# Bilinear samples on TensorE instead of VectorE for the first two chunks, and a convolution that follows its samples by thirds

## The chip, the cores and the metric

The kernel runs on one core of a Trainium2 chip. The metric is the device time of one execution in microseconds (us), as the median of several runs. A profile is one further execution, taken with the hardware profiler; the clock of the profile starts at the first instruction.

The core has five engines, each with its own queue that is worked off strictly in order. TensorE (PE in the views) multiplies matrices into PSUM; the loads of its stationary operands are listed apart as PEld. VectorE (DVE) does elementwise work and copies out of PSUM. ScalarE (ACT) computes exponentials. GpSimd (POOL) issues indirect DMAs here and computes a few small powers. SyncE (SP) issues nearly all other DMAs.

## The reference, cut to what matters

The input is four images of 128 channels and 64 x 64 pixels. Layer 0 is a deformable 3 x 3 convolution on the group-normalised image; the edited code is its sampling step:

```python
offset = conv2d(x, w_off, b_off)                    # 18 channels
mask = sigmoid(conv2d(x, w_mask, b_mask))           # 9 channels
py = base_y + ki + offset[:, 0::2];  px = base_x + kj + offset[:, 1::2]
y0 = floor(py);  x0 = floor(px);  wy = py - y0;  wx = px - x0
samples = (v00 * (1 - wy) * (1 - wx) + v01 * (1 - wy) * wx
           + v10 * wy * (1 - wx) + v11 * wy * wx) * mask   # v..: four corner pixels, 0 outside
x = x + einsum('bckhw,ock->bohw', samples, w_flat) + bias  # k: the 9 taps
```

Layer 1 takes the 4096 pixels of an image as tokens of 128 channels. It normalises them and runs an attention with 16 heads of 8 channels (queries, keys and values are the same ring products of cosines), a small feed-forward part, and a mixture of eight experts with the best two per token. Every token attends to all 4096 of its image:

```python
scores = einsum('bhsd,bhtd->bhst', q, q) / sqrt(8)
ctx = einsum('bhst,bhtd->bhsd', softmax(scores), q)
```

## The kernel before, in words

**Two streams.** The long part is attention, written as a list of steps (`steps`). One step takes 128 keys against 512 queries for a group of four heads: `scores` (L1261) puts a product in PSUM, ScalarE takes the exponential (L1270), and `context` (L1281) multiplies it with the values into `acc`. Beside it runs everything else, written as Python generators that yield what their next piece needs (`need`: TensorE time, VectorE time, a latency, whether it holds the PSUM bank, a time after which data have landed). A planner, the class `Beside`, keeps a modelled time for each engine and decides at build time in which order the pieces are put into the queues. The order of the instructions on TensorE, VectorE, SyncE and GpSimd is then exactly the order of emission (`tc.manual_schedule`). Before the first step is possible the planner is forced along (`force`); afterwards each attention step lets in as many pieces as fit (`step`).

**Preparation of an image.** An image has 8 chunks of 512 pixels, and a chunk has 4 blocks of 128. `prepare` loads the image, group-normalises it, writes a table of pixel pairs to DRAM (`corner_table`), computes offsets, indices `idx` and the four weights of each sample `wt` in two halves (`offsets`; the second half's index and weight part is the generator `rest`), and then runs `deform`.

**`deform`** (L599) walks over 96 units. A unit is one block and three of the nine taps; in a chunk the order is three taps for the four blocks, then the next three taps. Of each unit:

- `gather` (L625, three indirect DMAs on GpSimd) brings, for each tap, four corner pixels of 128 channels for each of 128 positions into the tile `v`. Up to unit 35 of image 0 gathers run four units ahead, with five buffers (three under the tag `v`, two under the tag `et`, taken by `spare`).
- L645: VectorE multiplies `v` with the weights `wt`, 1536 elements a partition. L650 and L651 add the four corners, 768 and 384 elements.
- In chunks 0 and 1 of image 0, TensorE transposes the three samples (L662) into a PSUM tile `sT_ps`, and VectorE copies it into `sT_first` (L665, the function `move`, emitted one unit later). In all other chunks VectorE transposes 32 x 32 blocks and the samples go through DRAM (`smd`, L686 and L698).

**`convolved`** (L719) follows when a chunk's twelve units are done: nine taps in two halves of 256 columns, each split into four matmuls of 32 output rows (`by_columns`, L281), added up in one PSUM tile `conv_ps`. Then come the bias and the residual `xr` (L758), a transposition, and `features`: layer norm statistics, a power on GpSimd (`rstd`, L396), the normalised tokens (L788), cosines and ring products on VectorE (L811 to L822), a copy on GpSimd (`fx`, L823), a transposition and a split in two parts (L836 to L839), and the DMAs that put keys, queries and values into DRAM, from where attention loads them. For image 0 attention begins as soon as chunk 0's tokens are there and goes on as further chunks come in.

**PSUM.** `misc` hands out one bank to all pieces, except while the list `alone` is filled, that is until chunk 0 is prepared and again at the very end; then it takes from the three buffers that scores use otherwise.

Of the kernel before, what the change touches and what calls it, by code (L numbers as in the profile page):

```python
# [9 lines left out]
F32 = mybir.dt.float32  # L10
# [3 lines left out]
ALU = mybir.AluOpType  # L14
# [8 lines left out]
P = 128  # L23
C = 128
# [6 lines left out]
KK = 9  # L31
# [16 lines left out]
NST = 3  # L48
# [151 lines left out]
FREE = -1.0  # L200


def need(pe=0.0, dve=0.0, lat=0.0, hold=False, after=0.0):

    return pe, dve, lat, hold, after


def ve(n, ops=1):  # L210

    return ops * (0.17 + n / 960.0)


MM256 = 0.44
MM128 = 0.23


def tr(n):

    return 0.13 + 0.115 * n
# [3 lines left out]
def kernel(  # L225
# [22 lines left out]
    nc = tc.nc  # L248
# [350 lines left out]
    def deform(b, tab, idx, wt, rest):  # L599
# [12 lines left out]
        def gather(last):  # L612

            nonlocal issued
            while issued < len(units) and issued <= last + (4 if early(issued) else 2):
# [12 lines left out]
                    )  # L628
                ahead.append((v, beside.gathered()))

        sent = 0.0
        moved = []
        gather(-1)
        for n, (ch, kg, j) in enumerate(units):
# [6 lines left out]
            v, landed = ahead.pop(0)  # L641
            v4 = v.rearrange("p k (q c) -> p (k q) c", c=C)
            w12 = wt[:, j, 3 * kg : 3 * kg + 3, :].rearrange("p k q -> p (k q)")
            yield need(dve=ve(1536), after=landed)
            nc.vector.tensor_tensor(v4, v4, w12[:, :, None].to_broadcast([P, 12, C]), ALU.mult)  # L645
            if moved:
                yield need(pe=0.01, dve=ve(384))
                moved.pop()()
            yield need(dve=ve(768) + ve(384))
            nc.vector.tensor_tensor(v[:, :, : 2 * C], v[:, :, : 2 * C], v[:, :, 2 * C :], ALU.add)  # L650
            nc.vector.tensor_tensor(v[:, :, :C], v[:, :, :C], v[:, :, C : 2 * C], ALU.add)  # L651
            if b == 0 and ch < 2:


                if n % 12 == 0:
                    while len(summed) < ch:
                        yield need(lat=0.5)
                    sT = big.tile([P, KK, CH], F32, tag="xs", name=f"sT_first{ch}")
                yield need(pe=tr(3), lat=FREE, hold=True)
                pt = misc(f"sT_ps{j}_{kg}")  # L660
                for k in range(3):
                    nc.tensor.transpose(pt[:, P * k : P * (k + 1)], v[:, k, :C], ident)  # L662

                def move(sT=sT, kg=kg, i=j % 4, pt=pt):
                    nc.vector.tensor_copy(  # L665
                        sT[:, 3 * kg : 3 * kg + 3, P * i : P * (i + 1)],
                        pt[:, : 3 * P].rearrange("p (k c) -> p k c", c=P),
                    )

                moved.append(move)  # L670
                beside.later(beside.now + 0.8, lambda n=n: gather(n))
                if n % 12 == 11:
                    yield need(pe=0.01, dve=ve(384))
                    moved.pop()()
                    featuring.append(True)
                    beside.add("prepare", convolved(b, ch, sT), 0.5, True)
                    if ch == 0:
                        yield from rest
                continue

            yield need(dve=ve(384))
            if j % 4 == 0:
                beside.flush(sent)
# [32 lines left out]
        while featuring:  # L716
            yield need(lat=1.0)

    def convolved(b, ch, sT=None):  # L719

        xr = work.tile([P, CH], F32, tag="p2", name=f"xr{b}_{ch}", bufs=NP2)
        nc.sync.dma_start(out=xr, in_=xf[b, :, CH * ch : CH * (ch + 1)])
# [13 lines left out]
        if not in_order:  # L736
# [1 line left out]
            yield need(lat=6.0)  # L738
            get(1)
            yield need(lat=4.0)  # L740
        for k in range(KK):
            if k == 2 and not in_order:
                get(2)
            for hf in range(2):
                last = k == KK - 1 and hf == 1
                yield need(pe=MM256, dve=ve(128, 4) if last else 0.0, lat=0.2 if last else FREE, hold=not last)
                if k == 0 and hf == 0:
                    po = misc(f"conv_ps{b}_{ch}")
                by_columns(
                    po[:, 256 * hf : 256 * (hf + 1)], wconv_sb[:, k, :],  # L750
                    sT[:, k, 256 * hf : 256 * (hf + 1)], k == 0 and hf == 0, last,
                )
# [815 lines left out]
```

## Time and profile before

| quantity | value |
|---|---|
| median of 3 runs | 7589.68 us (7587.77 to 7598.68) |
| profiled execution, time | 7632.52 us |
| its span, first to last instruction | 7630.7 us |
| busy PE, ACT, DVE, POOL | 93%, 90%, 59%, 22% of the span |
| first exponential | at 180.4 us |
| ScalarE busy, 200 to 400 us | 115 of 200 us |
| ScalarE busy, 700 to 900 us | 189 of 200 us |
| gathers, L625 | 1152, busy 1450.7 us |
| products, L645 | 384, mean 1735 ns |
| additions, L650 and L651 | 384 each, mean 956 and 562 ns |

In the page's groups a row gives line, engine, operation, output tile and input tiles, shapes, number, busy time, mean duration of one, and the idle time of the engine in front of them. In a timeline a row gives start, duration, engine, line, operation and number; the brackets hold the idle time ahead of it and what ended that. Two or more rows of one engine may be merged where they follow each other closely. Matmul records can be missing, so their numbers are lower bounds.

### The profile page before, as it was taken

To read this page: it belongs to the slowest core of one execution; us is meant where nothing else is said; L and a number is where in the kernel's file an instruction comes from. 1 tells how busy PE (TensorE), PEld (TensorE's weight loads), DVE (VectorE), ACT (ScalarE), POOL (GpSimd) and SP (SyncE) were. 2 spreads that over 40 slices of the span, in tenths; PEclk is the share of its full clock that TensorE was granted. 3 is DMA by queue.
4 is the path that set the end of the run, shared out by engine and by line. 5 is a ranking of instruction groups with operands and counts; after the bars stand their busy time and mean duration, and the time that the engine had idled before them with its cause. 6 is when DMAs were issued, how large, how long until landed. Compare 5 with 4: busy or idle time off the path is not lost.

```text
span 7630.7 us, 180510 instructions
## 1 busy us (share of the span) xinstructions
PE 7132.4 (93%) x73736; PEld 2383.1 (31%) x73736; DVE 4479.3 (59%) x8976; ACT 6855.1 (90%) x7441; POOL 1653.8 (22%) x1326
## 2 busy tenths in 40 slices
PE   3679899899999999999999999989999999999997
PEld 2122232223333333333333323323333333333333
DVE  6766356667444867776554677775444545455534
ACT  0569899899999999999999988989999999999995
POOL 5544034443000432422000334331000000000000
PEclk6889999999999999999999999999999999999998
DMA  6677567978445878887655688897554466667662
GB/s 176 208 212 222 137 209 238 302 235 295 151 172 196 289 231 268 282 273 239 203 179 185 232 274 287 286 309 251 184 175 162 148 232 230 234 217 244 222 204 64
DMA packets 909787, 1689.50 MB, mean 221 GB/s; under 512 B 150754, under 2 KB 384124, under 8 KB 858268
## 3 DMA queue, kind: packets, MB, share of 16 engines
q1 hardware_dynamic: 809102, 1371.37, 54.5%
q0 software_dynamic: 92160, 302.06, 12.5%
q8 instruction: 579, 9.49, 0.5%
q10 hardware_dynamic: 7694, 4.52, 0.2%
q14 instruction: 252, 2.06, 0.1%
HBM read 1027.51 MB, written 650.14 MB: 220 GB/s over the span
## 4 chain that ended last, share of the span: by engine, by line
PE 82%; DMA 8%; DVE 4%; issue 3%; ACT 2%; SPq 1%; POOL 1%; another core or an unknown queue 0%; ACTq 0%; POOLq 0%; DVEq 0%
PE acc L1281 40%; PE sc L1261 24%; PE acc L1214 5%; PE e_ps L281 4%; PE conv_ps L281 4%; DMA et<-etd 3%; PE f_ps L281 2%; ACT e L1270 2%; DMA sT<-smd 1%; PE om_ps L533 1%; DMA etd<-st 1%; DVE v L645 1%; DMA smd<-tr 1%; POOL v L625 0%; PE ao_ps L281 0%
## 5 line engine op out<-in xcount | busy, mean ns | idle before, releaser
L1270 ACT ACTIVATE e<-sc 128x1024 f32<-128x1024 f32 x7400 | 6852.0, 1076 | 637.9 <-PE sc L1261 456.3
L1281 PE MATMUL acc<-e,qf 128*9 128x512 f32 (+1 forms) x29600 | 3946.4, 602 | 33.8 <-DVE cu L1488 15.2
L1261 PE MATMUL sc<-qT,kT 32*128 32x512 f32 x14800 | 2380.9, 500 | 193.8 <-ACT e L1270 97.7
L1261 PEld LDWEIGHTS sc<-qT,kT 32*128 32x128 f32 x14800 | 948.2, 183 | 3663.1 <-ACT e L1270 3140.8
L625 POOL DMA_INDIRECT v<-tab,idx x1152 | 1450.7, 1259 | 1679.6 <-DVE tr L686 1058.0
L1140 DVE STREAM_TRANSPOSE st<-e 128x1024 f32<-128x1024 f32 x792 | 937.3, 1221 | 774.8 <-ACT e L1270 651.0
L1281 PEld LDWEIGHTS acc<-e,qf 128*9 128x9 f32 (+1 forms) x29600 | 682.3, 91 | 629.3 <-issue 345.8
L396 POOL TENSOR_TENSOR r<-ln_t,expo 128x4 f32<-128x4 f32 x96 | 112.2, 1170 | 3111.0 <-DVE ln_t L394 3073.8
L645 DVE TENSOR_TENSOR v<-v,wt 128x1536 f32<-128x1536 f32 x384 | 666.1, 1735 | 102.9 <-DMA v<-tab,idx 88.2
L1214 PE MATMUL acc<-et,qv 128*9 128x128 f32 x12672 | 509.2, 277 | 58.9 <-DMA et<-etd 45.5
L1065 DVE TENSOR_TENSOR eo<-e_ps,gt 128x512 f32<-128x512 f32 x256 | 175.2, 686 | 549.1 <-PE e_ps L281 540.3
L650 DVE TENSOR_TENSOR v<-v 128x768 f32<-128x768 f32 x384 | 367.1, 956 | 9.8
L281 PE MATMUL conv_ps<-sT,wconv_sb 128*32 128x256 f32 x4320 | 352.3, 400 | 11.0 <-DMA sT<-smd 8.8
L1214 PEld LDWEIGHTS acc<-et,qv 128*9 128x9 f32 x12672 | 270.8, 90 | 263.2 <-issue 220.9
L1486 DVE COPY cu<-acc 128x512 f32<-128x512 f32 x128 | 88.5, 691 | 349.0 <-PE acc L1281 290.5
L686 DVE STREAM_TRANSPOSE tr<-v 128x128 f32<-128x128 f32 x1080 | 249.3, 281 | 45.2 <-DMA etd<-st 36.5
L651 DVE TENSOR_TENSOR v<-v 128x384 f32<-128x384 f32 x384 | 215.7, 562 | 13.3
L396 POOL TENSOR_TENSOR rstd<-lt_t,expo 128x4 f32<-128x4 f32 x32 | 59.4, 1856 | 515.2 <-DVE lt_t L394 494.9
L281 PE MATMUL f_ps<-w_sb,h 128*32 128x128 f32 x4096 | 167.6, 282 | 1.5 <-issue 1.5
L950 DVE TENSOR_SCALAR h<-h_ps,b_sb 128x512 f32<-128x512 f32 x128 | 94.9, 744 | 100.3 <-PE h_ps L948 85.0
L823 POOL COPY fx<-rn 128x512 f32<-128x512 f32 x32 | 26.9, 840 | 535.2 <-DVE rn L822 338.2
L965 DVE TENSOR_TENSOR a<-a,f_ps 128x512 f32<-128x512 f32 x32 | 22.0, 686 | 202.9 <-PE f_ps L281 202.5
(224 smaller groups left out, 3148.5 us busy)
## 6 DMA issues: line engine op xcount, KB each, us to landing
etd<-st SPq DMA_DIRECT2D x396, 1024.0 KB
et<-etd SPq DMA_DIRECT2D x396, 1024.0 KB
kT<-kTd SPq DMA_DIRECT2D x372, 256.0 KB
smd<-tr SPq DMA_DIRECT2D x360, 192.0 KB
sT<-smd SPq DMA_DIRECT2D x360, 192.0 KB
qT<-qTd SPq DMA_DIRECT2D x166, 256.0 KB
atd<-cu SPq DMA_DIRECT2D x128, 256.0 KB
qf<-fqd SPq DMA_DIRECT2D x372, 72.0 KB
```

The lines of the kernel that those rows point to most:

```text
L281: nc.tensor.matmul(dst[c : c + 32], lhsT=lhsT[:, c : c + 32], rhs=rhs, start=start, stop=stop)
L625: nc.gpsimd.indirect_dma_start(out=v[:, k, :], out_offset=None, in_=tab, in_offset=bass.IndirectOffsetOnAxis(ap=idx[:, j, kk : kk + 1], ax ...
L645: nc.vector.tensor_tensor(v4, v4, w12[:, :, None].to_broadcast([P, 12, C]), ALU.mult)
L650: nc.vector.tensor_tensor(v[:, :, : 2 * C], v[:, :, : 2 * C], v[:, :, 2 * C :], ALU.add)
L651: nc.vector.tensor_tensor(v[:, :, :C], v[:, :, :C], v[:, :, C : 2 * C], ALU.add)
L686: nc.vector.transpose(out=tr9[:, k, :, j % 4, :], in_=v[:, k, :C].rearrange("p (c i) -> p c i", i=32),)
L1065: nc.vector.tensor_tensor(ws[hf], pe.rearrange("p (e c) -> p e c", c=C), gt[:, i, 4 * hf : 4 * (hf + 1), None].to_broadcast([P, 4, C]), AL ...
L1140: nc.vector.transpose(out=st[:, :, 2 * pr : 2 * pr + 2, :].rearrange("p o h (q j) -> p o (h q) j", j=32), in_=es[pr].rearrange("p h (q o i ...
L1214: nc.tensor.matmul(acc[32 * h : 32 * h + QW, P * kt : P * (kt + 1)], lhsT=qv[:, at : at + QW], rhs=e[:, :, h, 32 * t : 32 * (t + 1)], star ...
L1261: nc.tensor.matmul(ps[i // 2][:, i % 2, :], lhsT=kT[h : h + 32, P * (t % 4) : P * (t % 4 + 1)], rhs=qT[h : h + 32, :], start=True, stop=True,)
L1270: nc.scalar.activation(e, ps[pr], AF.Exp, scale=1.0 / math.sqrt(HD))
L1281: nc.tensor.matmul(acc[32 * h : 32 * h + width, :], lhsT=flat[:, first : first + width], rhs=es[h // 2][:, h % 2, :], start=(t == ts[0]), ...
```

## The change

For units 0 to 23 (image 0, chunks 0 and 1) VectorE no longer multiplies and adds the corners. It builds twelve diagonal matrices `dg`, identity times one corner's weights, in one instruction of 1536 elements; the tile has the tag `st` with three buffers. TensorE multiplies each corner's pixels with its diagonal matrix and adds the four corners of a tap in PSUM; the product comes out transposed already. Each of these multiplications is split in four column strips by `by_columns`.

In chunk 0 the convolution is taken out of `convolved` and goes along in thirds (`taps`): when three taps of all four blocks are copied, their six multiplications are emitted, into a PSUM tile `conv_first` that is held from unit 0 on. Chunk 1 keeps its convolution in one piece at the end. The generator `rest` is run after unit 5 rather than after unit 11.

```diff
+        def taps(sT, kg):
+            for k in range(3 * kg, 3 * kg + 3):
+                for hf in range(2):
+                    yield need(pe=MM256, lat=FREE, hold=None)
+                    half = slice(256 * hf, 256 * (hf + 1))
+                    by_columns(
+                        po[:, half], wconv_sb[:, k, :], sT[:, k, half],
+                        k == 0 and hf == 0, k == KK - 1 and hf == 1,
+                    )
...
-            yield need(dve=ve(1536), after=landed)
-            nc.vector.tensor_tensor(v4, v4, w12[:, :, None].to_broadcast([P, 12, C]), ALU.mult)
+            first = b == 0 and ch < 2
+            if first:
+                yield need(dve=ve(1536))
+                dg = work.tile([P, 4, 4, P], F32, tag="st", name=f"dg{j}_{kg}", bufs=NST)
+                dg = dg.rearrange("p r h x -> p (r h) x")[:, :12]
+                nc.vector.tensor_tensor(
+                    dg, ident[:, None, :].to_broadcast([P, 12, P]),
+                    w12[:, :, None].to_broadcast([P, 12, P]), ALU.mult,
+                )
+            else:
+                yield need(dve=ve(1536), after=landed)
+                nc.vector.tensor_tensor(v4, v4, w12[:, :, None].to_broadcast([P, 12, C]), ALU.mult)
             if moved:
                 yield need(pe=0.01, dve=ve(384))
                 moved.pop()()
-            yield need(dve=ve(768) + ve(384))
-            nc.vector.tensor_tensor(v[:, :, : 2 * C], v[:, :, : 2 * C], v[:, :, 2 * C :], ALU.add)
-            nc.vector.tensor_tensor(v[:, :, :C], v[:, :, :C], v[:, :, C : 2 * C], ALU.add)
-            if b == 0 and ch < 2:
+                if ch == 0 and j % 4 == 0:
+                    yield from taps(sT, kg - 1)
+            if first:
                 if n % 12 == 0:
                     while len(summed) < ch:
                         yield need(lat=0.5)
                     sT = big.tile([P, KK, CH], F32, tag="xs", name=f"sT_first{ch}")
-                yield need(pe=tr(3), lat=FREE, hold=True)
-                pt = misc(f"sT_ps{j}_{kg}")
+                    if ch == 0:
+                        po = misc("conv_first")
                 for k in range(3):
-                    nc.tensor.transpose(pt[:, P * k : P * (k + 1)], v[:, k, :C], ident)
+                    yield need(pe=4 * MM128, lat=FREE, hold=True, after=landed)
+                    if k == 0:
+                        pt = misc(f"sT_ps{j}_{kg}")
+                    for q in range(4):
+                        by_columns(
+                            pt[:, P * k : P * (k + 1)], v4[:, 4 * k + q], dg[:, 4 * k + q],
+                            q == 0, q == 3,
+                        )
...
                 beside.later(beside.now + 0.8, lambda n=n: gather(n))
+                if n == 5:
+                    yield from rest
                 if n % 12 == 11:
                     yield need(pe=0.01, dve=ve(384))
                     moved.pop()()
+                    if ch == 0:
+                        yield from taps(sT, kg)
                     featuring.append(True)
-                    beside.add("prepare", convolved(b, ch, sT), 0.5, True)
-                    if ch == 0:
-                        yield from rest
+                    beside.add("prepare", convolved(b, ch, sT, po if ch == 0 else None), 0.5, True)
                 continue
+            yield need(dve=ve(768) + ve(384))
+            nc.vector.tensor_tensor(v[:, :, : 2 * C], v[:, :, : 2 * C], v[:, :, 2 * C :], ALU.add)
+            nc.vector.tensor_tensor(v[:, :, :C], v[:, :, :C], v[:, :, C : 2 * C], ALU.add)
...
-    def convolved(b, ch, sT=None):
+    def convolved(b, ch, sT=None, po=None):
...
-        for k in range(KK):
+        if po is not None:
+            yield need(pe=0.01, dve=ve(128, 4), lat=0.2)
+        for k in range(KK) if po is None else ():
```

## The prediction

> **What bounds the kernel now.** I read the page first: its slices, then its groups.
>
> ```profile
> ACT  0569899899999999999999988989999999999995
> ...
> L625 POOL DMA_INDIRECT v<-tab,idx x1152 | 1450.7, 1259 | 1679.6 <-DVE tr L686 1058.0
> ```
>
> A slice is 191 us. From the fifth on ScalarE and TensorE are full; nothing edited here runs there. What can move is the hole at the start. The timeline of ScalarE shows where it starved (in brackets the idle time before a row):
>
> ```profile
> 180.42 5.61 ACT L1270 ACTIVATE e<-sc 128x1024 f32<-128x1024 f32 x6 [125.74 <-PE sc L1261]
> ...
> 272.33 5.60 ACT L1270 ACTIVATE e<-sc 128x1024 f32<-128x1024 f32 x6 [37.53 <-PE sc L1261]
> ...
> 513.08 5.60 ACT L1270 ACTIVATE e<-sc 128x1024 f32<-128x1024 f32 x6 [27.35 <-issue]
> ```
>
> Attention waits for chunk 0 (until 180), chunk 1 (272) and later, most at 382 (10.8) and 513. So long as it starves at 513, a preparation that is earlier by S shortens the whole by S, and attention that merely starts earlier gains nothing. Next, the timeline of one unit of chunk 0, all engines:
>
> ```profile
> 90.10 0.94 POOL L625 DMA_INDIRECT v<-tab,idx  x1 [0.30 <-issue]
> 91.03 1.76 DVE L645 TENSOR_TENSOR v<-v,wt 128x1536 f32<-128x1536 f32 x1 [1.46 <-DMA v<-tab,idx]
> 91.35 2.26 POOL L625 DMA_INDIRECT v<-tab,idx  x1 [0.31 <-issue]
> 92.70 0.55 DVE L665 COPY sT_first<-sT_ps 128x384 f32<-128x384 f32 x1
> 93.17 0.95 DVE L650 TENSOR_TENSOR v<-v 128x768 f32<-128x768 f32 x1
> 93.91 1.03 POOL L625 DMA_INDIRECT v<-tab,idx  x1 [0.30 <-issue]
> ...
> 94.81 0.88 PE L662 MATMUL sT_ps<-ident,v 128*128 128x128 f32 x3 [4.27 <-issue]
> ```
>
> GpSimd never pauses beyond its 0.30; VectorE waits 1.46 for the gathered rows. The gathers are the pace: 0.94 + 2.26 + 1.03 + 0.9 = 5.1 us a unit (mean 5.0). A gather that starts inside the 1.76 us product ends 0.82 after it, so each unit loses 1.25 against three free gathers at 1.25 each (0.95 + 0.30). Last, rows of the timeline after chunk 0's samples:
>
> ```profile
> 115.71 5.10 PE L281 MATMUL conv_ps<-sT_first,wconv_sb 128*32 128x256 f32 x62
> ...
> 131.99 1.13 DVE L758 SCALAR_TENSOR_TENSOR xr<-conv_ps,bconv_sb,xr 128x128 f32<-128x128 f32 x4 [5.52 <-PE sT_ps L662]
> ...
> 139.27 2.48 POOL L396 TENSOR_TENSOR rstd<-lt_t,expo 128x4 f32<-128x4 f32 x1 [1.74 <-DVE lt_t L394]
> ...
> 155.25 1.26 POOL L823 COPY fx<-rn 128x512 f32<-128x512 f32 x1 [13.50 <-DVE rn L822]
> ```
>
> The convolution takes until 131 and then features begin. Their two GpSimd instructions stand in the gathers' queue: between 137.5 and 156.7 no gather runs. So chunk 1's last gather ends at 189.25 = 50.16 + 24 x 5.0 + 19. Its rows land at 191.7, its last copy ends at 198.3, and its convolution runs from 198.3 to 221.6.
>
> **Part by part.** *VectorE, units 0 to 23.* Before: 1.76 + 0.95 + 0.56 + 0.55 = 3.8 us. After: 1.76 (same shape; identity times weights) + 0.55 = 2.3. The 36 us removed are no gain by themselves: in chunk 0 it waits for gathers anyway. The new product no longer waits for rows, only for one of three `st` buffers, that is for the matmuls three units back; the copy before it waits for TensorE, and behind it stand the next product and the features.
>
> *TensorE.* Three transposes (0.88) become 12 column-split calls. The recorded instructions are two to a matmul (chunk 0's convolution, 72 matmuls, has 144), so 8 to a call. The nearest rows of the same form, from image 0's later timeline:
>
> ```profile
> 2027.24 0.65 PE L281 MATMUL f_ps<-w_sb,h 128*32 128x128 f32 x16
> 2027.70 1.04 PE L1281 MATMUL acc<-e,qf 128*32 128x512 f32 x8
> ```
>
> Two calls take 0.46 us, so 0.23 a call and 12 x 0.23 = 2.8 us a unit at full clock. At half clock: three 256-column calls take 2.72 (198.34 to 201.06) against 1.31 (205.23 to 206.54), a factor 2.08, so 0.48 and 5.7 us. I take 2.8, because a busy stretch of this form lifts the clock: granted 0.51 in 116 to 118, 1.00 in 118 to 120; and full clock outlived idling from 193.1 to 196. Between units 2 us would stay idle. Thirds of the convolution add 6 x 0.44 = 2.6 after every fourth unit, or 0.7 a unit: 3.5 of 4.6 us, covered by the gathers.
> [...] The rows above show 0.46 us / 16 = 29 ns in four column strips, and the measurement decides.
> [...]
>
> *Gathers.* The product still stalls one gather a unit, now at the phase of the copy before it. Gather starts are 1.25 apart and the window is 1.76, so the stall lies between 0.5 and 1.3 (the rows of today). I take the middle, 0.9: 24 x (1.25 - 0.9) = 8.4 us earlier. Bounds: 0 and 24 x 1.25 = 30 (no stall).
>
> *Chunk 0's end.* From the last landing (111.1) to the bias at 132 today 20.9; after: 4 calls 0.9, copy 0.75 with its wait, last third 2.6, handover 0.2: 4.5. Features can start about 20 us earlier. Little of that counts: `rstd` stands behind gathers queued ahead (to unit 17 today), and `fx` behind 13.5 us of VectorE. The hole in the gathers stays, but it loses the 1.7 wait, and some of a unit's gathers (3.75) may slip into it. I take 4, from 0 to 8.
>
> *Weights of the second half* (`rest`) move from after chunk 0 to after unit 5: 7 us of VectorE (116.3 to 123.2) ahead of product 6 and copy 5. Cover: 2.3 us idle a unit, over 6 units 14. Gathers under them today took 0.95 to 1.22, so they hardly stall. Without that cover 7 us fall on chunk 0's features, not on the gathers. They serve chunk 4 onward only. `xr` is then allocated later; its load is issued by SP at 49.9 today, 60 us early, so that is free.
>
> *Chunk 1's end.* Landing to convolution 6.6 us today; after: last 4 calls 0.9, copy 0.75, one attention step ahead on TensorE 1.8: 3.4. Gain 3.2, from -3 (two steps, all 12 calls after the landing, since outside chunk 0's stage one PSUM bank serves all) to 5. Its convolution keeps its 18 calls; six ran at half clock (4.9 us against 2.6). A warmer TensorE gains 2, from 0 to 2.3.
>
> **Sum.** S = 8.4 + 4 + 3.2 + 2 = 17.6 us. Chunks 2 and 3 follow unchanged and starvation outlasts the shift, so all of it arrives; an order laid out anew may move it by some 8 either way. The profiled execution took 7632.5 (span 7630.7); it would become 7615. It stands 42.8 above the median of the runs; I carry the difference over: 7589.7 - 17.6 = 7572.
>
> **Rivals.**
> *The gathers keep their pace.* The same product with the same operands locks as long as today (1.25 a unit), and the hole keeps its length. For: GpSimd's queue was never idle in chunk 0. Against: the product leaves the phase of the landing, and two more stalling adds go. Left are 3.2 + 2 - 1 for a longer TensorE queue = 4 us: 7586.
> *Slower: TensorE becomes the pace at half clock.* If the gaps of each unit hold the clock at 0.50 as today (60 to 116), a unit costs 5.7 + 18 x 0.91 / 12 = 7.1: chunk 0 ends at 57 + 85 = 142. In chunk 1 5.7 + 0.75, for the copy in the single bank, is 6.45: 77 more, 219 against 198.3. That is 21 us late: 7611. It decides once a unit's matmuls exceed 5.0. For: 0.50 is what the stage shows today. Against: at half clock TensorE would be gapless, and gapless stretches went to 1.00 within 3 us.
>
> **How the numbers follow.** Forecast 0.70, gather rival 0.13, slower rival 0.17. A measurement of this kernel can tell about 0.2% (15.2 us) from no change. The forecast's own range is a gain of 5 to 30; two thirds of its chance lie above 15.2 (0.46), the rest, 0.24, within. The gather rival is within (0.13). Of the slower rival, 0.01 is a half-way case within, 0.16 beyond. Faster 0.46, same 0.38, slower 0.16. The low end is no stall at all with the hole partly filled: 30 + 4 + 5, so 7550. The high end takes in most of the slower rival: 7606.
>
> **What the next profile would show.** Right: GpSimd's gathers at 4.6 us a unit from 60 to 105; L645's successor with no wait for rows; TensorE clock near 1 from 62 on; the bias of chunk 0 near 112; first exponential near 160; chunk 1's bias near 205; the row at 513 near 496. Wrong: TensorE gapless at 0.5 and gathers waiting for buffers; or a bias at 112 with chunk 1's last gather still near 189, which would make it the gather rival. A gap after 600 that today lacks would mean that the order itself got worse.

## The result and the profile after

The changed kernel is slower: 7609.0 us (median of 18 runs) against 7582.0 for the kernel before, a ratio of 1.0037, 95% interval 1.0030 to 1.0044. The forecast was 7572 in a range of 7550 to 7606. The time falls on the slower rival's 7611, but, as will be seen, mostly not for its reason. It is partly luck too: the forecast started from 7589.7, a median of three runs, and the 18 runs beside the changed kernel gave 7582.0, so the loss is 27 us where that rival had 21. The profiled execution took 7598.2 us (span 7596.4). The page's slices and the gathers' group:

```profile
ACT  0469899899999999999999988989999999999995
...
L625 POOL DMA_INDIRECT v<-tab,idx x1152 | 1437.8, 1248 | 1664.0 <-DVE tr L715 1011.3
```

From the fifth slice on (760 us) ScalarE is as full as before; the second slice fell from 5 to 4. The gathers did get cheaper, 1248 ns on average instead of 1259. ScalarE's timeline shows where the start went:

```profile
194.94 5.61 ACT L1301 ACTIVATE e<-sc 128x1024 f32<-128x1024 f32 x6 [139.70 <-PE sc L1292]
...
304.99 5.60 ACT L1301 ACTIVATE e<-sc 128x1024 f32<-128x1024 f32 x6 [53.72 <-PE sc L1292]
...
529.77 5.60 ACT L1301 ACTIVATE e<-sc 128x1024 f32<-128x1024 f32 x6 [27.08 <-PE sc L1292]
```

The first exponential came 14.5 us later than before (180.42), chunk 1's attention 32.7 later (272.33) and the row that was at 513.08 still 16.7 later. One unit of chunk 0, all engines (weight loads left out):

```profile
85.67 0.56 DVE L690 COPY sT_first<-sT_ps 128x384 f32<-128x384 f32 x1 [2.84 <-PE sT_ps L281]
85.91 0.94 POOL L625 DMA_INDIRECT v<-tab,idx  x1 [1.00 <-PE sT_ps L281]
86.15 1.75 DVE L660 TENSOR_TENSOR dg<-ident,wt 128x1536 f32<-128x1536 f32 x1
87.15 1.56 POOL L625 DMA_INDIRECT v<-tab,idx  x1 [0.30 <-issue]
...
87.21 0.43 PE L281 MATMUL sT_ps<-dg,v 128*32 128x128 f32 x5 [0.17 <-issue]
...
89.57 0.44 PE L281 MATMUL sT_ps<-dg,v 128*32 128x128 f32 x5 [0.26 <-issue]
...
90.77 0.56 DVE L690 COPY sT_first<-sT_ps 128x384 f32<-128x384 f32 x1 [2.87 <-PE sT_ps L281]
91.00 0.95 POOL L625 DMA_INDIRECT v<-tab,idx  x1 [1.04 <-PE sT_ps L281]
```

VectorE now waits 2.84 us for TensorE and no longer for rows, and GpSimd waits 1.00 for TensorE to free a buffer: TensorE has become the pace, 5.10 us from copy to copy. The stalled gather takes 1.56 instead of 2.26, so the stall fell to 0.6 us, more than the 1.25 to 0.9 that was foreseen; it is lost in the wait for TensorE. And TensorE is not busy with it: it waits too, with the cause "issue", for nothing that the profile shows. TensorE's own timeline, first units and, at the end, two units of chunk 1 for comparison:

```profile
62.06 0.44 PE L281 MATMUL sT_ps<-dg,v 128*32 128x128 f32 x6 [0.29 <-issue]
62.79 0.44 PE L281 MATMUL sT_ps<-dg,v 128*32 128x128 f32 x5 [0.29 <-issue]
...
64.96 0.43 PE L281 MATMUL sT_ps<-dg,v 128*32 128x128 f32 x4 [0.99 <-issue]
...
146.40 4.09 PE L281 MATMUL sT_ps<-dg,v 128*32 128x128 f32 x96 [4.41 <-issue]
...
151.01 2.83 PE L281 MATMUL sT_ps<-dg,v 128*32 128x128 f32 x96
```

At 151 the 96 recorded matmuls of a unit take 2.83 us, as predicted; no gather runs there (the last ended at 142.7). At 62 five or six recorded matmuls come every 0.73 us or a multiple of it, and 12.8 us pass between the copies of units 0 and 1. In the table below these stalls are summed as **gaps**: distances of 0.3 to 1.6 us between the starts of two recorded matmuls of the interpolation that follow each other on TensorE. They are a lower bound: unit 0's last recorded matmul starts at 61.4, but the semaphore that its end raises came only at 67.8. The granted clock is not what holds TensorE back for long (windows of 20 us; after the length come the busy times of PE, PEld, DVE, ACT and POOL with their counts, then the granted clock, DMA's share and GB/s):

```profile
60.00:80.00 20.00, 11.52 (x134) 5.76 (x129) 2.22 (x2) 0.00 (x0) 12.24 (x13) 0.67 0.62 182
80.00:100.00 20.00, 16.90 (x411) 12.06 (x403) 9.34 (x13) 0.00 (x0) 12.35 (x12) 0.98 0.45 133
```

### The profile page after: what moved, and what is told of

It is laid out like the page before. It is cut to its first block, busy times and chain, and to the rows that moved or that the text cites. A ratio compares the mean times of both kernels' runs of the same rounds, so it can differ in the third digit from the quotient of the medians.

```text
span 7596.4 us, 184900 instructions
## 1 busy us (share of the span) xinstructions
PE 7166.4 (94%) x75968; PEld 2439.7 (32%) x75968; DVE 4445.7 (59%) x8928; ACT 6851.3 (90%) x7441; POOL 1641.0 (22%) x1326
## 4 chain that ended last, share of the span: by engine, by line
PE 84%; DMA 8%; DVE 3%; issue 2%; ACT 1%; SPq 1%; another core or an unknown queue 0%; POOL 0%; POOLq 0%; ACTq 0%; DVEq 0%
PE acc L1312 40%; PE sc L1292 25%; PE acc L1245 5%; PE e_ps L281 4%; PE conv_ps L281 3%; DMA et<-etd 2%; PE f_ps L281 2%; ACT e L1301 1%; PE sT_ps L281 1%; PE om_ps L533 1%; DMA etd<-st 1%; DMA sT<-smd 1%; DMA qT<-qTd 1%; DMA qTd<-loT 0%; PE ao_ps L281 0%
## 5 line engine op out<-in xcount | busy, mean ns | idle before, releaser
L1312 PE MATMUL acc<-e,qf 128*9 128x512 f32 (+1 forms) x29600 | 3923.1, 600 | 20.9 <-DVE cu L1517 9.7
L625 POOL DMA_INDIRECT v<-tab,idx x1152 | 1437.8, 1248 | 1664.0 <-DVE tr L715 1011.3
L666 DVE TENSOR_TENSOR v<-v,wt 128x1536 f32<-128x1536 f32 x360 | 624.0, 1733 | 83.8 <-DMA v<-tab,idx 75.2
L708 DVE TENSOR_TENSOR v<-v 128x768 f32<-128x768 f32 x360 | 344.6, 957 | 9.6
```

Of the source, the lines that this page charges most:

```text
L625: nc.gpsimd.indirect_dma_start(out=v[:, k, :], out_offset=None, in_=tab, in_offset=bass.IndirectOffsetOnAxis(ap=idx[:, j, kk : kk + 1], ax ...
L1312: nc.tensor.matmul(acc[32 * h : 32 * h + width, :], lhsT=flat[:, first : first + width], rhs=es[h // 2][:, h % 2, :], start=(t == ts[0]), ...
```

## Experiments

The theory to begin with (A) says that the number of TensorE's instructions, through the gaps, makes the units slow. Its rival (B) says that the streaming time in the array at half clock does. A third (C) put it down to the order copy, product, matmuls; two more came up on the way (D: what stands ahead in a queue; E: the gathers make the gaps).

The runs fell on chips of different speed, in sessions of several runs each, so a ratio compares runs of one session on one chip only. The kernel before tells the chips apart: 7462 and 7463 us on two faster ones, 7577 and 7610 in two sessions on a slower one, 7627 (one run) on another slower one. The table gives, for each profile, the kernel before's median in that session, the ratio with its interval, the mean distance of the copies of units 5 to 11, the gaps from 78 to 145 us, and the starts of chunk 1's last copy, of chunk 1's attention and of the 201st exponential (all in us).

| run | before | ratio (95%) | unit | gaps | last copy | attention 1 | 201st |
|---|---|---|---|---|---|---|---|
| e_before_c4 | 7610 | | 4.70 | | 199.1 | 269.5 | 478.1 |
| e_after_c4 | 7610 | 1.0031 (1.0020 to 1.0042) | 5.43 | 19.3 | 231.0 | 303.3 | 492.6 |
| e_full_c4 | 7610 | 1.0009 (0.9999 to 1.0019) | 3.50 | 2.0 | 216.8 | 288.0 | 481.5 |
| e_plain_loads | 7610 | one run | 3.82 | 1.5 | 212.6 | 284.9 | 481.5 |
| e_idle_gathers | 7627 | one run | 4.30 | 9.7 | 249.3 | 322.8 | 508.4 |
| e_pool_busy | 7627 | one run | 3.72 | 1.6 | 212.9 | 286.5 | 481.9 |
| e_after_again | 7577 | 1.0037 (1.0023 to 1.0051) | 5.43 | 16.0 | 232.5 | 305.8 | 493.6 |
| e_narrow | 7577 | 1.0019 (1.0007 to 1.0030) | 4.94 | 20.4 | 220.7 | 293.2 | 481.3 |
| e_no_thirds | 7577 | 1.0035 (1.0021 to 1.0049) | 5.05 | 19.3 | 225.6 | 297.7 | 485.5 |
| e_full_late | 7577 | 1.0022 (1.0010 to 1.0033) | 3.80 | 2.7 | 204.6 | 266.7 | 473.4 |
| e_before_again | 7463 | | 4.65 | | 193.0 | 257.0 | 456.8 |
| e_full_width | 7463 | 1.0006 (0.9996 to 1.0016) | 3.56 | 0.3 | 205.6 | 278.1 | 461.2 |
| e_two_corners | 7463 | 0.9997 (0.9988 to 1.0007) | 3.49 | 4.2 | 190.9 | 263.2 | 448.2 |
| e_thirds_alone | 7463 | 1.0026 (1.0013 to 1.0038) | 4.65 | | 201.6 | 288.5 | 479.2 |
| e_before_third | 7462 | | 4.65 | | 192.8 | 257.0 | 459.7 |
| e_full_again | 7462 | 1.0002 (0.9993 to 1.0011) | 3.56 | 0.3 | 205.6 | 277.9 | 462.2 |
| e_thirds_rest5 | 7462 | 0.9994 (0.9984 to 1.0004) | 3.81 | | 191.2 | 266.0 | 453.9 |
| e_hybrid | 7462 | 0.9996 (0.9987 to 1.0004) | 4.09 | 1.3 | 191.6 | 267.1 | 455.7 |

### The two kernels again

No edit in these five runs.

> The kernel before, unchanged, for a second profile: the one shown took 7632.5 us, 34 us above the slowest of the other runs, so stretches after 700 us can't be compared with the changed kernel's. Every theory: 7567 to 7599 us, first exponential near 180.4, chunk 1's attention near 272.3, the row at 513 near 513, as in the first profile (the start is the same, the excess lies later). If the row at 513 moves by over 5 us, start times from one profile are no measure of the change.

> The kernel before once more, for a profile beside the next three. In two profiles so far chunk 1's attention began at 272.3 (span 7630.7) and at 257.0 (span 7458.9, a faster chip; 261 if stretched by the ratio of the two chips' medians, 1.016). If the first was unlucky at the start (its two convolutions stalled 19 us in gaps with the cause issue, the second's 7.3), this one shows 261 to 265 on the slower chip or 255 to 259 on the faster; if the start is what the chip makes of it, 270 to 274 on the slower.

> The kernel before, for a profile on the chip of the next three. On the chip of 7462 us: chunk 1's attention at 257 again (two profiles there agree within 1 us). On the chip of 7577 us: 261 to 265 if the first profile's 272 was a disturbed start, 270 to 274 if that chip's start is slower by itself.

> The changed kernel, unchanged, on the same chip as the experiments (the last four ran on a chip on which the kernel before took 7463 us, 1.6% less than in the first comparison, so differences must be taken within a call). Every theory: slower than the kernel before by 20 to 34 us (27 at first), chunk 0's bias near 140 and chunk 1's near 250; if the difference vanishes on a faster chip, the comparison of the other runs with the first result falls.

> The changed kernel, unchanged. Theory A (the column-split calls' issue gaps set the pace of the units): slower than before by 20 to 34 us on either chip, gaps of 0.25 to 1.6 us inside its streams before 260 us sum to 40 to 50 us, chunk 0's bias 15 to 25 us later than with full width. If on the faster chip it is within 8 us of before, the loss belongs to one chip, and what tells the two chips apart is the cause to look for.

The start repeats itself: chunk 1's attention of the kernel before at 257.0 in both profiles of the faster chips, at 272.3 and 269.5 in the two of slower chips, so that start was no accident of one profile. The row at 513.08 was at 513.06 in e_before_c4, but at 491.5 and 493.8 on the faster chips, so start times too are compared on one chip only. The loss repeats (28 and 27 us in the medians), but it is shown for slower chips alone: the changed kernel never fell on a faster one.

### Fewer instructions: full width

```
-    by_columns(pt[:, P*k : P*(k+1)], v4[:, 4*k + q], dg[:, 4*k + q], q == 0, q == 3)
+    nc.tensor.matmul(pt[:, P*k : P*(k+1)], lhsT=v4[:, 4*k + q],
+                     rhs=dg[:, 4*k + q], start=q == 0, stop=q == 3)
```

> The changed kernel, but each of the 12 products of a unit is one full-width matmul instead of four calls of 32 columns: a quarter of TensorE's instructions (48 recorded a unit instead of 192), the same sums. Theory A (instruction supply: dense streams of short column-split calls outrun what brings their instructions, which shows as idle time with the cause issue and instruction fetches close together): idle gaps of over 0.3 us inside the interpolation's matmuls, 44.7 us before chunk 0's features in the changed kernel, fall below 12; chunk 0's bias near 122 instead of 143.5, and the kernel at 7575 to 7590 instead of 7609. Theory B (the array's own time at a half clock is the pace, gaps are only gaps): a full-width call costs 0.29 us cold as one of the three transposes of before (0.88 for 3), or twice that; 3.5 us a unit gives the same times as theory A, 7.0 us gives a unit of over 7 us, a bias at 145 or later and 7611 or more, without gaps. So a bias at 122 with the gaps gone speaks for A, a bias at 145 or later with no gaps for B, and gaps that stay (over 30 us) speak against A whatever the time.

> The changed kernel with full-width matmuls once more, since the first time fell on the faster chip, where it was as fast as the kernel before (ratio 1.0006), while the same with later attention gave 1.0022 on the slower one. If full width takes back all but 2 us of the change's 27 on either chip: within 8 us of before. If it takes back only a part, and the faster chip hid the rest: slower by 10 to 20 us, and the number of instructions explains no more than half of the loss.

> The changed kernel with full-width matmuls, on the same chip. Theory A: 15 us or more faster than the changed kernel, within 8 us of the kernel before, gaps under 15 us. If the instruction count explains only a part: 5 to 12 us faster than the changed kernel.

Gaps from 78 to 145 us fell from 16 to 19 us to 2.0 or less, and chunk 0's bias came at 115.8 (faster chip) and 128.5 (slower; 142.0 with column-split calls, 13.5 us later where 15 to 25 were expected). On the slower chip 16 of 27 us came back: 7609.7 for the kernel before, 7620.6 with full width, 7637.0 as changed. The 10.9 us that are left exceed theory A's bound of 8. On the faster chips full width is within 2 us of the kernel before. In e_full_width GpSimd paused no longer than its 0.30 between 50 and 131 us. The time of a unit's matmuls in a dense stretch was no shorter; TensorE's timeline of the first full-width run:

```profile
155.40 2.94 PE L684 MATMUL sT_ps<-dg,v 128*128 128x128 f32 x24 [0.65 <-DVE sT_first L690]
158.99 2.94 PE L684 MATMUL sT_ps<-dg,v 128*128 128x128 f32 x24 [0.65 <-DVE sT_first L690]
171.62 1.22 PE L1292 MATMUL sc<-qT,kT 32*128 32x512 f32 x6 [9.68 <-DMA kT<-kTd]
```

2.94 us a unit, against 2.83 column-split in the changed kernel at 151 (granted clock 1.00). So it is not the streaming that was saved, but the gaps. The last row shows the next wait: the first attention step stands in the queue after four units of chunk 1 and waits 9.68 us for its keys, with the next unit behind it.

On the slower chip chunk 0's bias waits for something else. VectorE's timeline of e_full_c4:

```profile
128.49 1.12 DVE L789 SCALAR_TENSOR_TENSOR xr<-conv_first,bconv_sb,xr 128x128 f32<-128x128 f32 x4 [11.85 <-remote]
```

The last recorded matmul of the convolution began at 118.7 and `xr` had been loaded by 60, yet the bias came 9.8 us later (15.5 in e_full_late, on the same chip); in e_full_width it waited 2.49, for the convolution alone. The wait ended with an update, at 128.47, of a semaphore that only TensorE's matmuls raise, so the end of the convolution itself came late against its records (the ends of matmuls are modelled in the profile); why is not shown. It makes up most of the 12.7 us between 115.8 and 128.5. In the profiles of the two faster chips no such delay of over 1 us stands from 50 to 160 us; on the slower ones it also meets unit 0 of every run with four column-split corners, by 6 to 12 us. So on the slower chip the gaps are not all that TensorE lost, and full width did not remove all of it.

### Half the work, and the same instructions with fewer columns

```
-    for q in range(4): by_columns(..., q == 0, q == 3)     # after
+    for q in range(2): by_columns(..., q == 0, q == 1)     # e_two_corners
+    cut = P if q == 0 else 32                              # e_narrow
+    by_columns(pt[:, P*k : P*k + cut], v4[:, 4*k + q], dg[:, 4*k + q, :cut], q == 0, q == 3)
```

> The changed kernel with two of the four corners left out of the sums of chunks 0 and 1 (its output is not the reference's): half of the interpolation's matmuls, everything else, the weights' product included, as in the changed kernel. If TensorE is the pace of a unit (theories A and B): unit period falls from 5.1 or more to the gathers' 4.6 to 5.0, chunk 0's bias from 143.5 to near 118, and the kernel to 7575 to 7590. If the pace is the order of the steps (copy, product and matmuls waiting for each other, theory C), only the 2.6 us less of matmuls per unit at half clock come off some of the units: bias 130 to 138, kernel 7595 to 7605.

> The changed kernel with the same 48 column-split calls a unit in the same order (192 recorded instructions), but three of the four corners stream only 32 of 128 columns of the diagonal matrix (its output is not the reference's): the columns that stream through the array fall from 12 x 128 to 3 x 128 + 9 x 32 a unit, to 44%, the number of instructions stays. Theory A (the number of instructions issued sets the pace): gaps with the cause issue stay near 40 us, the first two units take over 8 us each, bias of chunk 0 at 135 to 145, kernel slower than before by 15 to 30 us. Theory B (streaming time, with the half clock, sets the pace): units become as cheap as with two corners left out, bias near 113 to 118, kernel within 8 us of before.

With half of the calls the kernel is as fast as before, on a faster chip, where the changed kernel itself was not run; chunk 0's bias came at 113.4, and theory C had 130 to 138. Cutting the streamed columns to 44% at the same number of calls left chunk 0 as slow as theory A had it: gaps 20.4 us, the units still 4.94 apart, bias at 138.4. Yet half of the time came back (14 of 28 us, just under A's bound), most of it in chunk 1: its last copy comes 11.8 us earlier than in e_after_again, the bias of chunk 0 only 4.4. So in chunk 1 the columns do count. All engines of e_narrow, one unit:

```profile
82.90 0.34 PE L281 MATMUL sT_ps<-dg,v 128*32 128x32 f32 x5 [0.38 <-issue]
83.61 1.61 PE L281 MATMUL sT_ps<-dg,v 128*32 128x32 f32 x52 [0.38 <-issue]
83.98 0.56 DVE L691 COPY sT_first<-sT_ps 128x384 f32<-128x384 f32 x1 [2.74 <-PE sT_ps L281]
...
87.88 0.35 PE L281 MATMUL sT_ps<-dg,v 128*32 128x32 f32 x5 [0.41 <-issue]
88.60 0.34 PE L281 MATMUL sT_ps<-dg,v 128*32 128x32 f32 x4 [0.37 <-issue]
...
88.97 0.56 DVE L691 COPY sT_first<-sT_ps 128x384 f32<-128x384 f32 x1 [2.77 <-PE sT_ps L281]
```

The matmuls are shorter (0.34 for five), but the bursts start as far apart, 0.72 us, and the unit is 4.99 us long. Streaming time, B's cause, does not set the pace of chunk 0's units.

### The gathers taken away, and put back idle

```
+    if b == 0 and 6 <= n < 24:                             # e_plain_loads
+        nc.sync.dma_start(out=v, in_=tab[: 6*P].rearrange("(k p r) c -> p k (r c)", p=P, r=2))
-    for k in range(3): nc.gpsimd.indirect_dma_start(out=v[:, k, :], ...)
+        for k in range(3):                                 # e_idle_gathers, besides
+            nc.gpsimd.indirect_dma_start(out=dum, ...)     # two buffers, nobody reads
+        for k in range(4): nc.gpsimd.memset(dum, float(k)) # e_pool_busy, instead
```

> The changed kernel, but from unit 6 to unit 23 the rows come by one plain load a unit on SyncE's queue (384 fixed rows of the same size, so its output is not the reference's); GpSimd then issues no gathers from 68 us to the end of chunk 1. TensorE's and VectorE's work is the same. Theory A (a dense stream of short calls stalls by itself): units 6 to 11 stay 4.5 us or more apart and the gaps between 80 and 140 us sum to over 12 us (22 in the changed kernel). Theory E (the gathers beside it make the gaps): units 6 to 11 come 2.6 to 3.6 us apart, gaps there under 4 us, chunk 0's bias near 110.

> The run with plain loads, and beside it the three gathers of each of units 6 to 23 into a scratch tile of two buffers that nobody reads or waits for (its output is not the reference's; twice the bytes move). Theory E1 (gathers in flight disturb TensorE's issue): gaps come back, the interpolation's gaps between 100 and 140 us sum to over 8 us and units 6 to 11 are 4 us or more apart though their rows are there. Theory E2 (in the changed kernel TensorE waits for the gathered rows or their buffers without the profile showing it): gaps stay under 4 us and units 2.6 to 3.2 us apart.

> The run with plain loads, and beside it four fills of 128 x 512 by GpSimd for each of units 6 to 23, into a scratch tile that nobody reads (output not the reference's). If a busy GpSimd by itself disturbs TensorE: gaps between 100 and 140 us over 4 us. If it is the gathers' transfers or their issue: gaps as in the run with plain loads, 1 to 3 us, units 6 to 11 at 2.6 to 2.9 us.

Without gathers the column-split stream runs as the prediction had priced it. All engines of e_plain_loads (DMA and weight loads left out):

```profile
110.24 8.46 PE L281 MATMUL sT_ps<-dg,v 128*32 128x128 f32 x299
...
113.11 0.56 DVE L694 COPY sT_first<-sT_ps 128x384 f32<-128x384 f32 x1 [3.44 <-PE sT_ps L281]
...
115.73 0.56 DVE L694 COPY sT_first<-sT_ps 128x384 f32<-128x384 f32 x1 [0.40 <-PE sT_ps L281]
...
118.35 0.56 DVE L694 COPY sT_first<-sT_ps 128x384 f32<-128x384 f32 x1 [0.40 <-PE sT_ps L281]
```

299 matmuls ran in 8.46 us without a gap, and three units in a row are 2.62 us apart. The mean of units 5 to 11 is 3.82, since the second half's weights and a third of the convolution stand between others. Until unit 6, where the gathers still run, its gaps (11.1 us before 78) are those of the changed kernel (10.8); unit 0's copy came only at 73.0 (61.0 in e_full_width), and so chunk 0's bias at 125.9 and not near 110.

The idle gathers were fewer, 23 from 78 to 140 us against 32 in the changed kernel, since two scratch buffers held them up, and 9.7 us of gaps came back, half of the changed kernel's. In the window that the expectation named (100 to 140 us) it was 3.4 us, against 11.4 in e_after_c4 and 0.8 with plain loads: under theory E2's bound of 4, while the units, 4.30 apart, are on theory E1's side. The trace of e_after_c4 settles E2: by the packets of the gathers' queue (80 to a gather) all rows of unit 11 had landed at 115.9, and its matmuls, from 131.5 to 137.0, still show 2.8 us of gaps. So they did not wait for rows. The rows around one of the idle gathers:

```profile
82.44 1.31 POOL L627 DMA_INDIRECT dum<-tab,idx  x1 [0.35 <-issue]
...
82.50 0.41 PE L281 MATMUL sT_ps<-dg,v 128*32 128x128 f32 x4 [0.21 <-issue]
83.24 0.43 PE L281 MATMUL sT_ps<-dg,v 128*32 128x128 f32 x6 [0.33 <-issue]
...
83.98 3.39 PE L281 MATMUL sT_ps<-dg,v 128*32 128x128 f32 x116 [0.31 <-issue]
```

The bursts of four and six begin under the gather, and the dense stretch of 116 begins with no gather running. Over the whole stage the tie is looser: from 78 to 145 us a gather is executing on GpSimd in 52% of the time in gaps and in 39% of the time in dense streams (65% and 47% in e_after_c4). GpSimd's fills brought nothing back: 1.6 us of gaps in all, and 0.7 from 78 to 101.5, where 44 of the fills ran and e_after_c4 has 8.0 (in the window that the expectation named hardly any ran). So without gathers beside it the dense stream of short matmuls has hardly any gaps here (1.5 us), and some come back with gathers that nobody waits for (9.7); a GpSimd that fills memory adds next to none (1.6). In time, one run each, it was 7613 us with plain loads (7610 for the kernel before and 7637 as changed in that session), 7647 with idle gathers and 7623 with the fills (7627 for the kernel before). What of a gather does it stays open, and since the rows move twice beside the idle gathers (1703.9 MB in the whole run against 1689.8 with plain loads alone), the traffic may have a part in what came back.

### The parts alone

```
 # e_no_thirds: after, without taps(); convolved(b, ch, sT) as before
 # e_thirds_alone: taps() and po, but product, adds and transposes as before, rest after chunk 0
 # e_thirds_rest5: the same, with
+    if n == 5: yield from rest
```

> The other part of the change alone: interpolation on TensorE with column-split calls and the second half's weights after unit 5, but chunk 0's convolution in one piece after its samples, as before. If all of the loss is the interpolation's pace (its columns took back 32 us between two and four corners): the thirds are worth their 10 us in chunk 0's bias, which comes 5 to 12 us later than in the changed kernel, and the kernel is slower than before by 27 to 40 us. If the thirds cost time as they did alone (19 us, through an order in which chunk 1's bias stood behind five units of chunk 2 on VectorE): slower than before by 5 to 20 us only.

> One part of the change alone: the first convolution follows chunk 0's samples by thirds, while the interpolation (VectorE's product and two adds, three transposes) and the place of the second half's weights stay as before. If the interpolation on TensorE alone did the harm (all theories): chunk 0's gathers end where they did before (109 to 111), the bias of chunk 0 comes 12 to 16 us earlier than before's 132 (convolution 15.3 us less one third), the first exponential earlier by as much, and the kernel is at 7575 to 7590: the same or up to 8 us faster, since rstd waits in the gathers' queue. If the thirds do harm of their own (each third queued ahead of the transposes), chunk 1's first attention row is later than 272 and the kernel is slower by 5 us or more.

> The change without the interpolation: convolution of chunk 0 by thirds and the second half's weights after unit 5, interpolation as before. With the weights left after chunk 0 the thirds alone were 19 us slower, since chunk 0's features then ran to their end ahead of chunk 1's first unit, and chunk 1's bias stood behind seven units of chunk 2 on VectorE. With the weights moved, the planned order has three units ahead of that bias, as before. Theory D (order was the harm): chunk 0's bias near 120, chunk 1's attention 5 to 12 us earlier than before's, kernel the same or up to 10 us faster. If the thirds themselves harm (they delay the transposes in TensorE's queue): slower by over 8 us again.

Without thirds the kernel is as slow as with them (26.8 and 28.3 us), and chunk 0's bias comes at the same 142.6 (142.8), where 5 to 12 us later was expected: its last copy (134.5) is 3.8 us earlier, and from there the whole convolution takes 8.1 us instead of 4.5 for a last third. Where TensorE is the pace, as here, work moved ahead on it was no gain. The thirds alone were 19 us slower for another reason. TensorE's timeline of e_thirds_alone:

```profile
209.62 5.35 PE L281 MATMUL conv_ps<-sT_first,wconv_sb 128*32 128x256 f32 x96
233.72 1.09 PE L782 MATMUL x_ps<-ident,xr 128*128 128x128 f32 x4 [18.75 <-issue]
```

and VectorE's:

```profile
226.91 1.72 DVE L657 TENSOR_TENSOR v<-v,wt 128x1536 f32<-128x1536 f32 x1
...
230.87 1.72 DVE L657 TENSOR_TENSOR v<-v,wt 128x1536 f32<-128x1536 f32 x1
232.50 1.12 DVE L775 SCALAR_TENSOR_TENSOR xr<-conv_ps,bconv_sb,xr 128x128 f32<-128x128 f32 x4
```

Chunk 1's convolution ended at 215.0, but its bias stands behind products of chunk 2 in VectorE's order and starts at 232.5. With the second half's weights moved to unit 5, three such products stand ahead instead of seven, and the kernel is as fast as before. Chunk 1's attention still came 9 us later than before's (266.0 against 257.0) where 5 to 12 us earlier was expected; the 201st exponential is 5.8 us earlier.

### Two attempts at a better version

```
-    prepared[b, ch] = beside.dve + 9.0                      # e_full_late, with full width
+    prepared[b, ch] = beside.dve + (26.0 if (b, ch) == (0, 0) else 9.0)
-    if first:                                               # e_hybrid, with full width
+    if first and ch == 0:        # chunk 1: product, two adds, three transposes as before
```

> The changed kernel with full-width matmuls, and the first attention step put into TensorE's queue after 7 units of chunk 1 instead of after 4 (the order's due time for chunk 0's keys set 17 us later). In the full-width run TensorE stood 9.7 us at 161.9 to 171.6 waiting for the keys' DMA with unit 17's matmuls behind it, and then took 5.2 us a unit between attention steps instead of 3.6. Theory D (with the calls cheap, what is left over is lost behind that wait): the last copy of chunk 1 comes at 184 to 192 instead of 205.6, chunk 1's attention at 258 to 266 instead of 278, and the kernel is 8 to 18 us faster than before. If the wait only moves (TensorE's queue then waits for VectorE or for gathers), the last copy stays over 198 and the kernel within 6 us of before.

> Chunk 0 as in the changed kernel with full-width matmuls and thirds; chunk 1 interpolated as before (product and two adds on VectorE, three transposes), since beside attention TensorE is the scarce engine and VectorE is not: chunk 1's units took 3.6 us before, and 3.6 to 6 with the sums on TensorE. Expected from the rows of both: chunk 0's bias 8 to 12 us earlier than before's, chunk 1's units at before's pace, so its attention 5 to 10 us earlier than before's and the kernel 3 to 10 us faster. If what the change loses is lost in chunk 0 or through the order that is laid out anew, this is no faster than full width in both.

Later attention removed the wait for keys (chunk 1's units came 3.6 us apart up to 182), but the last copy stayed at 204.6, since the three remaining units, now beside attention, took 8.4, 9.2 and 5.0 us. The kernel is 18.5 us slower than before, outside both expectations. Its profile is ahead of e_before_c4's (same chip, other session) up to the 1001st exponential (1316 against 1328). By an estimate from the two sessions' medians of the kernel before (7577 and 7610), some 6 of these 12 us are the sessions' difference; where the rest goes is not found. The hybrid is 4 us ahead at the 201st exponential, though chunk 1's attention came 10 us later than before's and not 5 to 10 earlier, and it cannot be told from the kernel before in time. Nothing tried beats it measurably.

## Why the prediction was wrong

**The step that failed** is TensorE's term: "3.5 of 4.6 us, covered by the gathers". The price of the calls was right where no gather runs (2.83 us for a unit at 151 us; 299 matmuls in 8.46 us in e_plain_loads, 28 ns each against the 29 estimated). It came from rows at 2027 us, and in that profile no gather runs from 1990 to 2070; the cover was taken to be passive. It is not: beside gathers the same calls took a unit to 5.43 us on average, above the gathers' own pace (4.70 in e_before_c4), and 12.8 for the second unit. Between the copies of the unit shown at 85.67 it is 5.10 us for 96 matmuls, 53 ns each, gaps included. The profile before had rows with the same neighbours: the column-split convolution of chunk 0, of which the prediction shows the first row, goes on like this on TensorE, beside gathers:

```profile
121.14 0.65 PE L281 MATMUL conv_ps<-sT_first,wconv_sb 128*32 128x256 f32 x4 [0.33 <-issue]
122.59 1.10 PE L281 MATMUL conv_ps<-sT_first,wconv_sb 128*32 128x256 f32 x3 [0.81 <-issue]
124.04 0.41 PE L281 MATMUL conv_ps<-sT_first,wconv_sb 128*32 128x256 f32 x2 [0.34 <-issue]
```

These are the same bursts, 0.72 us or twice that apart. On the faster chips this convolution has none beside the same gathers (144 matmuls in 10.3 us in e_before_again), while the interpolation with half of the calls has 4.2 us of gaps there (e_two_corners); how much the changed kernel would lose on them is open. On the slower chips, removing the gathers, or three quarters of the instructions, brought the gaps after 78 us from 19.3 us to 1.5 and 2.0 (one chip); that it takes both is shown, how they make them is not. By the full-width run they are worth some 16 of the 27 us. What makes the other 11 is not shown; the late end of the convolution and the wait for keys are candidates.

**Gathers.** The product's stall fell further than predicted, to 0.6 us; at three gathers of 1.25 and this stall a unit would be 4.4 us. The full-width runs show what it was worth: from the first gather to the 36th 56.0 us against 55.5 before, nothing (54.1 against 56.0 on the slower chip). There the stalls fell on other gathers (1.8 to 2.4 us each), now under copies and products in quick succession. On the faster chip the gather rival was right on this point.

**Chunk 0's end.** "The bias of chunk 0 near 112": 143.5 as changed, 115.8 with full width on the faster chip, 125.4 there before. From the landing of the last rows (109.6 in both, by the packets of the gathers' queue) it takes 6.2 us to the bias with full width, near the 4.5 predicted, but in the kernel before 15.8 on that chip and not 20.9, since its convolution has no gaps there. So the 20 us were 10.

**The hole and the features' queue.** "The hole loses the 1.7 wait, I take 4": in the changed kernel two holes came in its place, before `rstd` (11.21) and before `fx` (9.74). With full width on the faster chip there is one at that place, and it shrank from 13.50 to 9.73, about the 4 us predicted.

**Weights of the second half.** Their 7 us of VectorE had "14 us of cover". In e_full_width the copies around them are 9.3 us apart instead of 2.7, so some 6 us showed in TensorE's stream; GpSimd did not pause. Moving them is what keeps the order whole (e_thirds_rest5 against e_thirds_alone), which the prediction did not see.

**Clock.** "Near 1 from 62 on": 0.67 from 60 to 80, 0.98 from 80 to 100. The slower rival took half clock throughout; it had chunk 0's end at 142 and the time at 7611 nearly right, through gaps that it did not know.

**S against the end.** The start accounts for 14.5 us at the 201st exponential (492.6 against 478.1, one session), the medians differ by 27.3. In the same two profiles the 1001st exponential is 10.3 us later. But these executions were 12.8 above (before) and 11.4 below (changed) their medians, so the rest cannot be placed by them; "all of it arrives" is neither shown nor refuted.

## What to carry to other kernels

Work moved onto an idle engine has to be priced beside the traffic that runs there (a unit's calls took 2.83 us alone; beside gathers the units came 5.43 apart): take the price from rows with the same neighbours, which the profile before may already hold, or change the neighbours for one run and see. Where an engine will become nearly full, count instructions and not only columns: the same sums in a quarter of the instructions gave 16 of 27 us back (e_full_c4). And where an order is laid out ahead for in-order queues, a part that is ready earlier can put a wait for a transfer, or another chunk's work, in front of the next one (9.68 us for keys in e_full_width; a bias that started 17.5 us after its convolution's end in e_thirds_alone); look at what stands ahead of it there, not at the durations alone.

## What the runs showed of the hardware

In the first chunks, on the slower chips, dense streams of column-split matmuls beside GpSimd's gathers fell into bursts of one to six recorded matmuls every 0.72 us or a multiple of it; alone they ran at 28 ns a matmul (299 in 8.46 us in e_plain_loads). The instruction fetches that the profile records are no simple explanation: in the changed kernel, between 58 and 141 us, each took 0.9 to 1.6 us and they are 4.7 to 14.5 us apart, while one stall lasted from 61 to 77; in e_plain_loads they came as close as 3.5 us (108.5 and 112.0) in a stretch without a gap. A unit of twelve full-width matmuls took about as long as one of twelve column-split calls: 2.94 us in e_full_width (at 155.4) against 2.83 in the changed kernel (at 151.0, granted clock 1.00). After an idle stretch the first unit took 4.01 in e_full_late (at 156.4; the next ones 2.94) and 4.09 in the changed kernel (at 146.4, where the granted clock was 0.50 until 149.0 and then 1.00). The chips differ by 1.5 to 2.2% in the time of the kernel before (7462 to 7627 us), and one chip by 0.4% between sessions (7577 and 7610).
